# Three edits to the order of work in a two-layer decoder kernel: slot pieces before a routing product, cell transposes one step later, transpose before output in the causal end

## The chip, the cores and the metric

The kernel runs on one core of one Trainium2 chip. The metric is the device time of one execution in microseconds (us), the median of several runs; lower is better. The core has five engines that run side by side and wait for each other through semaphores: PE (TensorE, with its weight loads shown apart as PEld), DVE (VectorE), ACT (ScalarE), POOL (GpSimd) and SP (SyncE, which issues transfers).

## The reference, cut to what matters

Two sequences of 1024 tokens with 256 features (`x`, 16 tiles of 128 tokens) go through two decoder layers. Each of the six blocks adds its result to `x`:

```python
x = x + L0_attn(layernorm(x))            # linear attention and a feed-forward part
x = x + L0_xattn(ctx, layernorm(x))      # queries from x, keys from a context and x itself ("latent")
x = x + L0_ffn(layernorm(x))             # a gated cell scanned over the 2 sequences: "cell"
x = x + L1_attn(layernorm(x))            # causal attention, 16 heads
x = x + L1_xattn(layernorm(x), ctx)      # cross attention, 16 heads
x = x + L1_ffn(layernorm(x))             # 8 experts, top 2 of them per token, at most 64 places per
                                         # group of 256 tokens and expert
```

In the cell, a step is `f*c + i*g` with `f, i = sigmoid(x @ w.T + c @ u.T + b)` and `g = tanh(...)`; its input `x` has to stand feature-major (features on partitions), so the normed rows are transposed first. In the causal block, the attention sums are divided by the sum of the weights and multiplied by `Wout`. In the last block a router (a 256x8 product) gives eight logits per token; softmax, top 2 and a running count per expert then give each token a slot with its experts.

## The kernel before, in words

The stages follow each other in one program: linear attention with its feed-forward part, latent attention, cell, causal attention, cross attention, experts. Wherever it matters here the order of instructions is written out by hand: within `tc.manual_schedule()` each engine takes its instructions in the order in which the Python code issues them (a few short DVE instructions are moved among their neighbours in the build), and generators are stepped against each other so that one stage's side work stands between the steps of another. A wait at the head of an engine's queue holds all that stands behind it on that engine. PSUM tiles come from rings: `k.s()` (two banks each, three of them in the latent, cross and first expert stages, two in the scan), `k.t()` (one bank; three of them in the causal stage); a tile that is taken waits until the tile that had its bank before has been read.

**Cell.norm (L1341 to L1359)** prepares four tiles of 128 tokens for the cell: bn_stats, bn_aggr and a power on POOL (step 1), four `ln_apply` on DVE (L219, step 2), then eight 128x128 transposes on PE (L1355) into one `k.s()` tile and two copies out of it, one on DVE (L1357) and one on ACT (L1358). Each `yield` ends a step. Groups 0 and 1 (the first sequence) run through `Cell.ahead` as the side work of the last unit of latent attention (`Latent.run`, unit 3: `side = following`, one `next(side)` after each of 18 attend steps). An attend step is scores (L1237, with L1226 and L1230 for the context) on PE, an exponential on ACT (L1244), a running sum on DVE (L1249; in the first half of unit 3 always on DVE), and a product (L1164) of an earlier step on PE. Groups 2 and 3 run in `Cell.scan`, one `next(side)` after each of the twelve gates of `Cell.gates` (L1403: four matmuls, then an activation on ACT, L1408; after each three gates DVE combines them, L1414 and L1415). The second sequence's gates (L1439) read groups 2 and 3.

**Causal.finish (L1959 to L2003)** takes each tile t of 128 tokens through three stages: `divide` (four transposes L1968 on PE, reciprocal L1973 and product L1975 on DVE), `turn` (two transposes L1983, copy `yT` L1985 on ACT) and `out` (the product with `wo`, L1991, and the addition to `x` on DVE, L1996). The loop at its end staggers the stages. Each stage is one step of `side` between the attend steps of `Causal.run`; the last four tiles of the second sequence are drained at the end of `Causal.run` with nothing between them. `y` has three buffers, `yT` two.

**CROSS_ORDER (L2071 to L2092)** is a string that names, step by step, the work of the cross attention, with the routing steps of the experts mixed in, and `FIRST_ORDER` (L2477) goes on with the first expert's work. Their names are: `route_<step>_u`, the routing of four tiles, u = 0 to 3: norm, transposes L2600 (`route_turn`), copy `xT` (`route_xT`, L159 on ACT), router product L2608 (`route_prod`), copy of the logits' line (`route_line`), its transposes L2617 (`route_back`), copy into `lg` (`route_copy`, L161 on DVE when the name ends in '); `choose_b`, ten steps that place the tokens of sequence b (L2635 to L2713); `up`, `gelu`, `mul`, a slice of the first expert's hidden layer (L3021 on PE, L3043 on ACT, L3047 on DVE); `scatter_0`, which brings the tokens to their slots. The last two steps of `choose` are 16 short DVE instructions, from `kept` (L2696) to `gate_of` (L2713). The `xT` of routing unit 3 comes from a pool (`moe_route`) that is opened after the pool of the cross attention has been closed and takes its memory, which held the tiles that `choose_0` works on and the `xT` of routing unit 2.

Of the kernel before, what the change touches and what calls it, by code (L numbers as in the profile page):

```python
# [327 lines left out]
class Linear:  # L328
# [79 lines left out]
    def norm(self, g):  # L408
        xh = self.rows4("xh", g)
        for i in range(4):  # L410
            self.k.ln_apply(
                xh[:, i * D : (i + 1) * D], self.group(g)[:, i, :], self.of["mv", g], self.of["r2", g], i
            )
# [286 lines left out]
class Latent:  # L700
# [555 lines left out]
    def finish(self, b):  # L1256

        k, nc, x = self.k, self.k.nc, self.x
        for j in range(2):
            s = k.s()  # L1260
            for i in range(4):
                for c in range(DC):
                    nc.tensor.matmul(
                        s[:, i * D : (i + 1) * D],
                        lhsT=self.oT[(b, j)][:, c, i * P : (i + 1) * P],
                        rhs=self.w["wo"][:, c, :],
                        start=(c == 0),
                        stop=(c == DC - 1),
                    )
            four = x[:, b * TB + 4 * j : b * TB + 4 * j + 4, :]  # L1270
            nc.vector.tensor_tensor(four, four, s.rearrange("p (t d) -> p t d", t=4), ALU.add)
            yield

    def run(self, late, following):
# [43 lines left out]
        drain(side)  # L1318
        finish = self.finish(1)
        next(finish)  # L1320
        self.divide()
        drain(finish)


class Cell:
# [15 lines left out]
    def norm(self, g):  # L1341

        k, nc = self.k, self.k.nc
        rows = lambda i: self.x[:, 4 * g + i, :]
        mv, r = k.ln_stats(rows, 4)
        yield
        xh = self.rows()
        for i in range(4):
            k.ln_apply(xh[:, i, :], rows(i), mv, r, i)
        yield  # L1350
        s = k.s()
        for kc in range(DC):
            for i in range(4):
                at = (kc * 4 + i) * P
                nc.tensor.transpose(s[:, at : at + P], xh[:, i, kc * P : (kc + 1) * P], k.ident)  # L1355
        dst, half = self.xT[g // 2], g % 2 * 512
        nc.vector.tensor_copy(dst[:, 0, half : half + 512], s[:, :512])  # L1357
        nc.scalar.copy(dst[:, 1, half : half + 512], s[:, 512:])  # L1358
        yield  # L1359
# [152 lines left out]
class Causal:  # L1512
# [446 lines left out]
    def finish(self, b, tiles):  # L1959

        k, nc, x = self.k, self.k.nc, self.x
        late = self.late
        ys = {}

        def divide(t):
            s = k.t()
            for grp in range(4):
                nc.tensor.transpose(  # L1968
                    s[:, grp * P : (grp + 1) * P], self.oS[b, t // 4][:, grp, t % 4 * P : (t % 4 + 1) * P], k.ident
                )  # L1970
            s3 = s.rearrange("p (h d) -> p h d", d=32)
            rd = k.small([P, 16], "rd")
            nc.vector.reciprocal(rd, s3[:, :, AUG])  # L1973
            y = ys[t] = late.tile([P, D], F32, tag="y", bufs=3, name="y")
            nc.vector.tensor_tensor(  # L1975
                y.rearrange("p (h d) -> p h d", d=16), s3[:, :, :16], rd.unsqueeze(2).to_broadcast([P, 16, 16]), ALU.mult
            )

        def turn(t):
            y = ys[t]  # L1980
            s = k.t()
            for c in range(DC):
                nc.tensor.transpose(s[:, c * P : (c + 1) * P], y[:, c * P : (c + 1) * P], k.ident)  # L1983
            yT = ys[t] = late.tile([P, D], F32, tag="yT", bufs=2, name="yT")
            nc.scalar.copy(yT, s[:, :D])  # L1985

        def out(t):
            yT = ys.pop(t)
            s = k.t()
            for c in range(DC):  # L1990
                nc.tensor.matmul(  # L1991
                    s[:, :D], lhsT=yT[:, c * P : (c + 1) * P], rhs=self.w["wo"][:, c, :],
                    start=(c == 0), stop=(c == DC - 1),
                )
            one = x[:, b * TB + t, :]
            nc.vector.tensor_tensor(one, one, s[:, :D], ALU.add)  # L1996

        for i in range(len(tiles) + 3):
            for stage, do in ((3, out), (2, turn), (0, divide)):
                if 0 <= i - stage < len(tiles):  # L2000
                    do(tiles[i - stage])
                    yield
# [83 lines left out]
ones_01 sum_3 ones_03 add_2 val_3 inv_3 route_stat_21 route_stat_20 spr_3 os_3 route_mean_2 disp_00  # L2086
route_root_2 yT_3 route_shift_2 route_norm_21' out_3 ones_05 ones_07 route_norm_20' ones_06 ones_04
put_00 disp_01 add_3 route_turn_2 route_stat_31 put_01 route_stat_30 route_xT_2 route_mean_3 up_2
route_root_3 route_prod_2 route_shift_3 route_norm_30' route_norm_31 route_line_2 up_1 route_turn_3
route_back_2 route_copy_2' choose_0 choose_0  # L2090
"""


class Cross:
# [245 lines left out]
    def rows(self, u):  # L2340
        rows = self.tile(u, "mrows", [P, DC, 512], BF16)
        self.k.copy(rows.rearrange("p c n -> p (c n)"), self.of.pop(("m_t", u)))
# [969 lines left out]
```

## Time and profile before

| What | us |
|---|---|
| median of 3 runs | 1535.53 (1532.67 to 1536.07) |
| the profiled execution: its own time | 1539.67 |
| its span in the trace | 1537.70 |
| PE busy in the span | 1498.8 |
| DVE, ACT, POOL busy | 822.1, 502.8, 285.2 |

The profiled execution is one run of its own, 4.1 us above the median of the others; 2.0 us of its time lie outside the span. All durations of the text come from it. A row of the timeline gives start and busy time in us, engine, line, operation, tiles, the number of instructions, and in brackets how long the engine stood idle before the row and what released it. A row of the waits gives the total in us, the number of times and the longest. A row of the windows gives, for a stretch of time, the busy time of PE, PEld, DVE, ACT and POOL, then the clock that PE was granted (1.00 is full speed), the busy share of the DMA engines and GB/s.

### The profile page before, as it was taken

What the parts mean: (1) busy time and instruction counts of PE and PEld (TensorE: products, weight loads), DVE (VectorE), ACT (ScalarE), POOL (GpSimd) and SP (SyncE); (2) the same over time, 40 slices, a digit from 0 to 9 for tenths busy, and PEclk for the clock granted to TensorE, in tenths of its full rate; (3) what the DMA queues carried; (4) which work ended last, traced back from release to release, by engine and by line L of the source; (5) the groups of instructions that cost most, each with busy time, mean ns of one, the idle gap of its engine ahead of it and who ended that gap; (6) DMA issues with size and microseconds to landing.
All of it is one profiled execution on the core that took longest, in us unless ns stands there. A gap on an engine that the chain in (4) does not pass through costs nothing. (4 is left out here: it accounts for less than half of the span.)

```text
span 1537.7 us, 21255 instructions
## 1 busy us (share of the span) xinstructions
PE 1498.8 (97%) x8666; PEld 858.5 (56%) x8672; DVE 822.1 (53%) x1532; ACT 502.8 (33%) x769; POOL 285.2 (19%) x332
## 2 busy tenths in 40 slices
PE   9999999999999999999999999999988999999998
PEld 7765555444343344654444454455677476757786
DVE  6823453656654542587768678367651133343323
ACT  2222411433323332225566645644420111121110
POOL 2002310233212120531511111210033211101110
PEclk9999999999999999999999999999999999999999
DMA  6000000000000000011111111062013275343531
GB/s 260 1 3 1 1 0 0 1 0 1 1 1 0 1 31 1 0 36 56 56 55 56 56 36 60 17 232 63 2 48 129 81 251 193 104 166 122 178 106 56
DMA packets 61378, 94.79 MB, mean 62 GB/s; under 512 B 4616, under 2 KB 52808, under 8 KB 60872
## 3 DMA queue, kind: packets, MB, share of 16 engines
q1 hardware_dynamic: 56216, 80.89, 15.7%
q0 software_dynamic: 3808, 11.05, 2.0%
q8 instruction: 95, 1.56, 0.4%
q10 hardware_dynamic: 1232, 1.07, 0.2%
q14 instruction: 27, 0.22, 0.0%
HBM read 64.13 MB, written 28.87 MB: 60 GB/s over the span
## 5 line engine op out<-in xcount | busy, mean ns | idle before, releaser
L3021 PE MATMUL ps_s<-xe,w 128*128 128x352 f32 (+9 forms) x616 | 171.8, 440 | 0.0
L1951 ACT ACTIVATE pT<-ps_t 128x512 f32<-128x512 f32 x244 | 132.5, 595 | 103.7 <-PE ps_t L1885 103.6
L1768 PE MATMUL ps_s<-kT,qT 32*128 32x512 f32 (+3 forms) x768 | 152.5, 519 | 4.0 <-DVE mneg L1802 2.5
L3047 DVE TENSOR_TENSOR hid<-ga,ps_s 128x512 f32<-128x512 f32 (+3 forms) x99 | 62.0, 628 | 175.8 <-ACT ga L3043 171.5
L1885 PE MATMUL ps_t<-qT,kT 32*128 32x512 f32 (+3 forms) x656 | 150.8, 515 | 0.0
L3060 PE MATMUL ps_o<-wo,hid 128*128 128x256 f32 (+1 forms) x638 | 142.4, 383 | 3.2 <-DVE hid L3047 2.7
L3021 PEld LDWEIGHTS ps_s<-xe,w 128*128 128x128 f32 (+1 forms) x616 | 108.5, 187 | 61.2 <-issue 30.5
L3060 PEld LDWEIGHTS ps_o<-wo,hid 128*128 128x128 f32 (+1 forms) x638 | 121.2, 192 | 22.1 <-DVE hid L3047 3.2
L3043 ACT ACTIVATE ga<-ps_s 128x512 f32<-128x512 f32 (+3 forms) x99 | 54.0, 549 | 207.6 <-PE ps_s L3021 193.6
L1120 DVE TENSOR_REDUCE part<-ps_s 128x2 f32<-128x1024 f32 x64 | 77.3, 1220 | 61.0 <-PE ps_s L1110 60.4
L1244 ACT ACTIVATE pT<-ps_s 128x1024 f32<-128x1024 f32 x64 | 65.5, 1024 | 112.7 <-PE ps_s L1237 112.7
L1802 DVE TENSOR_REDUCE part<-ps_s 128x2 f32<-128x1024 f32 x64 | 77.9, 1221 | 30.0 <-PE ps_t L1885 25.3
L1768 PEld LDWEIGHTS ps_s<-kT,qT 32*128 32x128 f32 x768 | 59.6, 183 | 58.7 <-issue 30.9
L1846 PE MATMUL ps_o<-pT,vr 128*32 128x256 f32 (+1 forms) x1280 | 90.0, 368 | 0.8 <-DVE oS L1861 0.8
L1898 POOL TENSOR_SCALAR_AFFINE_SELECT pT<-pT 128x512 f32<-128x512 f32 (+1 forms) x80 | 44.0, 553 | 231.2 <-ACT pT L1951 211.5
L1802 DVE TENSOR_REDUCE mneg<-ps_s 128x2 f32<-128x768 f32 (+2 forms) x96 | 80.5, 867 | 2.2
L3021 PE MATMUL ps_s<-xin,w 128*128 128x256 f32 (+3 forms) x264 | 78.2, 453 | 3.0 <-DVE hid L3047 3.0
L1249 POOL TENSOR_TENSOR acc<-acc,pT 128x1024 f32<-128x1024 f32 x21 | 49.3, 2349 | 156.9 <-ACT pT L1244 150.7
L1110 PE MATMUL ps_s<-kT,qT 64*128 64x512 f32 x256 | 70.3, 634 | 0.8 <-DVE part L1101 0.8
L1846 PEld LDWEIGHTS ps_o<-pT,vr 128*32 128x32 f32 x1280 | 27.2, 108 | 77.2 <-issue 64.7
L1885 PEld LDWEIGHTS ps_t<-qT,kT 32*128 32x128 f32 x656 | 67.0, 183 | 5.7 <-issue 1.8
L1237 PE MATMUL ps_s<-qT,kT 64*128 64x512 f32 x256 | 68.5, 612 | 1.0 <-DVE part L1120 1.0
(459 smaller groups left out, 2343.2 us busy)
## 6 DMA issues: line engine op xcount, KB each, us to landing
w<-in_w SPq DMA_DIRECT2D x32, 684.0 KB, 8.4
out_rows<-zero SPq DMA_DIRECT2D x7, 2048.0 KB, 7.5
got<-out_rows SPq DMA_DIRECT2D x28, 512.0 KB, 4.8
wo<-in_wo SPq DMA_DIRECT2D x8, 1280.0 KB, 7.0
xi_rows<-xin SPq DMA_DIRECT2D x1, 4112.0 KB
xr<-xi_rows POOLq DMA_DIRECT2D x6, 514.0 KB
w_ffn<-in_w_ffn SPq DMA_DIRECT2D x1, 2304.0 KB
w<-in_w_cell SPq DMA_DIRECT2D x2, 1024.0 KB, 19.1
```

What stands on the lines that cost most here:

```text
L1110: self.k.nc.tensor.matmul(s3[:, hh, :], lhsT=self.q[u][rows, qt * P : (qt + 1) * P], rhs=self.kt[u][rows, half * 512 : (half + 1) * 512], ...
L1120: self.k.nc.vector.tensor_reduce(self.part_of(u)[:, half, qt, :], s3, AX.X, ALU.max, negate=True)
L1237: nc.tensor.matmul(s3[:, hh, :], lhsT=self.ones_h[hr, :] if i else kt[hr, kk * P : (kk + 1) * P], rhs=rows[hr, cols] if i else q[hr, cols] ...
L1244: nc.scalar.activation(pT, s3, AF.Exp)
L1768: self.k.nc.tensor.matmul(s3[:, hh, at : at + n], lhsT=self.q[u][rows, qt * P : (qt + 1) * P], rhs=self.kt[u][rows, half * 512 : half * 51 ...
L1802: nc.vector.tensor_reduce(out, s3[:, :, at : at + n], AX.X, ALU.max, negate=True)
L1846: nc.tensor.matmul(self.o[hh * 32 : hh * 32 + 32, cols], lhsT=self.vr[b][:, kk, 4 * grp + hh, :], rhs=of(hh), start=fresh, stop=last and n ...
L1885: nc.tensor.matmul(out[:, at : at + n], lhsT=kt[rows, kk * P : (kk + 1) * P], rhs=q[rows, j * 512 + q0 : j * 512 + q0 + n], start=True, st ...
L1951: nc.scalar.activation(pT[:, hh, :], heads[hh], AF.Exp)
L3021: self.k.nc.tensor.matmul(cols(s[:m, i * 512 : (i + 1) * 512]), lhsT=wt[:, kc, at : at + m], rhs=cols(self.inputs[e][:, kc, first : 512]), ...
L3047: self.k.nc.vector.tensor_mul(self.hid[:m, hc, first : first + n], self.act.pop(hc)[:m, :n], self.now.pop(hc)[:m, 512 : 512 + n])
L3060: self.k.nc.tensor.matmul(o, lhsT=self.hid[:n, hc, st * P : (st + 1) * P], rhs=self.to[:n, hc, :], start=(hc == 0), stop=(hc == len(HCH) - 1),
```

## The change

Three places of the source change; nothing that is computed does, and the number of instructions on each engine stays the same.

1. `Cell.norm` has one more `yield`, so that the transposes come two steps after the `ln_apply` of their rows instead of one. Where two groups follow each other, all of the second group comes one step later, and its transposes two.
2. The loop at the end of `Causal.finish` takes `turn` before `out`: turn of tile i - 2, out of tile i - 3, divide of tile i.
3. In `CROSS_ORDER` the last two `choose_0` stand before `route_line_2`, ahead of `up_1`, `route_turn_3`, `route_back_2` and `route_copy_2'`, instead of behind them.

```diff
@@ Cell.norm
         for i in range(4):
             k.ln_apply(xh[:, i, :], rows(i), mv, r, i)
         yield
+        yield
         s = k.s()
@@ Causal.finish
         for i in range(len(tiles) + 3):
-            for stage, do in ((3, out), (2, turn), (0, divide)):
+            for stage, do in ((2, turn), (3, out), (0, divide)):
                 if 0 <= i - stage < len(tiles):
                     do(tiles[i - stage])
                     yield
@@ CROSS_ORDER
-route_root_3 route_prod_2 route_shift_3 route_norm_30' route_norm_31 route_line_2 up_1 route_turn_3
-route_back_2 route_copy_2' choose_0 choose_0
+route_root_3 route_prod_2 route_shift_3 route_norm_30' route_norm_31 choose_0 choose_0 route_line_2
+up_1 route_turn_3 route_back_2 route_copy_2'
```

Line numbers of the changed kernel are one higher than those given here from L1351 on.

## The prediction

> **What bounds the kernel now.** I read the page first, then PE's waits, then the timeline around each wait that the change touches. The page says that PE is busy in 97% of the span:
>
> ```profile
> PE 1498.8 (97%) x8666; PEld 858.5 (56%) x8672; DVE 822.1 (53%) x1532; ACT 502.8 (33%) x769; POOL 285.2 (19%) x332
> ...
> PE ps_t L2608 <- ACT xT L159: 4.3, 1, 4.3
> PE ps_s L3021 <- DVE hid L3047: 3.0, 1, 3.0
> PE ps_o L3060 <- DVE hid L3047: 2.7, 1, 2.7
> PE ps_s L1768 <- DVE mneg L1802: 2.5, 6, 0.8
> PE ps_s L1355 <- DVE xh L219: 2.5, 3, 1.3
> ...
> PE ps_t L1991 <- ACT yT L1985: 1.0, 2, 0.5
> ```
>
> The rows below the first are PE's waits in the whole span. So only what PE loses can be won: waits, and matmuls that run slowly because their operands arrive one by one. Three of these rows belong to the three edits: L2608 (router product), L1355 (cell transposes), L1991 (causal output).
>
> **Edit 1, the cell transposes.** Timeline, all in one kernel, the last row for comparison (eight transposes of another stage that wait for nothing between them):
>
> ```profile
> 509.42 1.64 PE L1355 MATMUL ps_s<-ident,xh 128*128 128x128 f32 x8 [0.85 <-DVE xh L219]
> ...
> 519.17 1.65 PE L1355 MATMUL ps_s<-ident,xh 128*128 128x128 f32 x8 [1.26 <-DVE xh L219]
> ...
> 561.74 1.54 PE L1355 MATMUL ps_s<-ident,xh 128*128 128x128 f32 x8
> ...
> 568.79 1.73 PE L1355 MATMUL ps_s<-ident,xh 128*128 128x128 f32 x8 [0.36 <-DVE xh L219]
> ...
> 1108.98 1.04 PE L2600 MATMUL ps_s<-ident,w 128*128 128x128 f32 x8
> ```
>
> Each group waits for the first of four DVE instructions (1.38 us together) and is then paced by the other three: 1.54 to 1.73 us where 1.04 are needed. One step later all four are done. An attend step takes PE 2.29 us (scores at 513.28 and 515.56 in the timeline), a gate 1.72 (four matmuls at 0.43). PE stood ready at 508.57, 517.91, 561.74 and 568.43 (start less wait), and DVE ended its four at 510.24, 520.00, 562.45 and 569.70: late by 1.67 and 2.09 against 2.29, and by 0.71 and 1.27 against 1.72. So all four waits go, the second with only 0.2 us to spare. Gain: 0.85 + 0.60, 1.26 + 0.61, 0.50, 0.36 + 0.69, sum **4.87**. What is late next: the two copies come behind one more running sum (1.22 us) on DVE, and the ACT copy holds the next exponential by some 0.6 us; PE does not need that exponential until a product one step on. A gate's copies stand behind two combining instructions (0.68 + 0.75); group 3 is ready four gates (6.9 us) before L1439 reads it. Bounds: 0 if the later place waits as long for something else, 4.9 at most. I take 4.9, because DVE is late by less than a step in all four rows and its other work keeps its place.
>
> **Edit 3, the slot pieces.** The rows of the L2608 wait, and the same four matmuls one unit earlier at the top:
>
> ```profile
> 1111.83 1.88 PE L2608 MATMUL ps_t<-xT,router 128*8 128x512 f32 x4
> ...
> 1116.44 0.41 PE L2617 MATMUL ps_t<-ident,xT 8*128 8x8 f32 x4
> ...
> 1119.61 0.22 DVE L2713 TENSOR_TENSOR gate_of<-m,m 128x64 f32<-128x64 f32 x1
> 1119.95 1.01 ACT L159 COPY xT<-ps_s 128x1024 f32<-128x1024 f32 x1 [5.57 <-DVE gate_of L2713]
> ...
> 1121.11 3.37 PE L2608 MATMUL ps_t<-xT,router 128*8 128x512 f32 x4 [4.26 <-ACT xT L159]
> ...
> 1124.41 1.59 PEld L3021 LDWEIGHTS ps_s<-xin,w 128*128 128x128 f32 x8 [1.50 <-issue]
> ```
>
> and of the windows
>
> ```profile
> 1122.00:1124.00 2.00, 2.00 (x4) 0.19 (x2) 0.75 (x2) 0.92 (x3) 0.00 (x0) 0.50 0.00 0
> ```
>
> PE is through with `route_back_2` (L2617) at 1116.85 and stands until 1121.11, because ACT's copy takes memory that `choose_0` still reads: `gate_of` is the last of it. The 16 pieces and four `at` instructions among them run from 1116.99 to 1119.83, 2.84 us, and waited only for the `lg` copy ahead of them in DVE's queue. Moved, they begin when DVE has normed unit 3 (two L219, 0.73 us together from 1111.74, done at 1112.47) and end at 1115.3. Then the copy's other wait comes last, the end of L2617 at 1116.85, since `xT` of unit 2 lay in the same memory. With the hand-overs of now (0.12 us to ACT, 0.15 to PE) PE begins L2608 at 1116.85 + 0.12 + 1.01 + 0.15 = 1118.13, 2.98 us earlier, and ends at 1120.01 if the four matmuls take 1.88. Now the next product starts at 1124.41: **4.40** gained, 2.98 of it wait and 1.42 speed. The speed is the clock: the windows row shows 0.50 granted behind this wait. If it falls all the same behind the 1.28 us that remain, the gain is 2.98; that is the lower end where the step works, and 4.4 the upper. I take 4.4, since the waits of 1.26 and 0.85 us above were followed by a clock of 1.00. [...]
>
> What the moved pieces push: on DVE only the `lg` copy (0.19 us, then ready at once at 1116.9); behind it `hid`, which waits for ACT anyway. ACT's table load (1.28) and two gelus follow its copy earlier by 3 us. No transfer is passed: POOL's and SP's queues have the same order in both builds; the scatter's POOL transfers begin earlier with their rows, SP's next weight loads wait for PE (L3021) and move with it.
>
> **Edit 2, transpose before output.** Between attend steps nothing shows: each stage is followed by a whole attend step of PE, and no wait of L1968, L1983 or L1991 stands in the loop; I take 0. In the drain the rows are
>
> ```profile
> 1011.15 1.13 PE L1991 MATMUL ps_t<-w,yT 128*128 128x256 f32 x4 [0.52 <-ACT yT L1985]
> ...
> 1013.02 1.13 PE L1991 MATMUL ps_t<-w,yT 128*128 128x256 f32 x4 [0.52 <-ACT yT L1985]
> ```
>
> where an output directly follows the transpose that feeds it; cross attention's first matmul follows at 1013.99. Behind the third divide (done at 1007.26) PE still has four outputs of 0.97 us from start to start, three turns of 0.22 and one divide of 0.52: 5.06, which would end at 1012.3. In the new order the first turn takes the PSUM bank of the turn before and waits for its ACT copy (1007.36), about 0.2; every other operand is ready a step earlier than needed. End 1012.6, gain **1.4** (0 to 1.7).
>
> **Sum.** 4.9 + 4.4 + 1.4 = 10.7 us. The profiled execution would take 1539.7 - 10.7 = 1529.0 (span 1527.0); the median of the runs, 4.1 below it, **1524.8**, which I predict as 1525. Under 0.2% (3.1 us) a measurement cannot tell from no change.
>
> **Rivals.**
> - *The expert stage gives edits 2 and 3 back.* PE waits there at 1157.07 (2.98) and 1168.95 (2.72, with half clock behind it), because ACT stands 5.34 and 3.14 us for something outside the engines ("remote"). If that event comes at a time of its own, PE reaches the wait earlier and stands longer: only 4.9 remain, 1530.6. Against it: POOL's and SP's transfers hang on DVE and PE and move along. The same rows can fall better: without these two waits and the half clock some 5 us more would go, 1520.
> - *The cell gain is not there*: the transposes wait in the new place too, for a DVE that is behind with its sums (1.22 us in every step of that half, plus statistics of 1.93 us, 1.40 + 0.36 + 0.17). 5.8 remain, 1529.7. Against it: DVE is busy 20.84 of the 40 us from 500.
> - *The clock falls behind the shorter wait too*: 1.4 less, 1526.2.
> - *Little is left*: both of the first two at once, under 3 us, 1533.
> - *Slower*: in the loop of causal attention a stage takes the bank that the stage before it leaves. Now divide waits for the addition L1996 (turn does so before), and turn for the division's product (output before). If DVE, which has a 1.23 us reduction in front of it in nearly every step, answers later than the next step begins, each of 12 tiles costs one such reduction, 14.8 us: 1539.3 against 1535.5. It decides from 0.9 us per tile. Against it: PE's waits show no such row in the loop now, although the banks are handed on at the same distance of one step.
>
> **How the numbers follow.** Forecast 0.69 (its own range 1522 to 1528: 1 us on each edit and 2 of scatter of the median of three). Expert stage takes it back 0.10, falls better 0.05; no cell gain 0.05; clock 0.04; little left 0.04; slower 0.03. Faster by over 0.2%: 0.69 + 0.10 + 0.05 + 0.05 + 0.04 = 0.93; same 0.04; slower 0.03. The range for 8 in 10 reaches from the better to the worse expert stage, 1520 to 1531.
>
> **What would show it.** Edit 1: four groups of L1356 at about 1.04 us without a wait. Edit 3: the copy of `xT` released by PE L2618, L2609 at 1.88 us after a wait near 1.3, clock 1.00. Edit 2: no wait of L1992 for `yT`, cross attention's first matmul 1.4 us sooner after the last `oS` copy. It is wrong if PE's busy time and waits fall by 10 us up to 1125 but the end moves less (the expert stage), or if new waits stand at L1969, L1984 or L1992 between the attend steps.

## The result, and the profile after

The changed kernel takes 1522.13 us (median of 4 runs, 1521.57 to 1524.38) against 1535.40 of the kernel before beside it (4 runs): ratio 0.9923, 95% interval 0.991 to 0.9935, or 11.8 us (10.0 to 13.8). The medians lie 13.3 us apart. Predicted were 1525.0 us and 10.7 us. The profiled execution after took 1524.38 us, its span 1522.3 against 1537.7: 15.4 us. Where the span fell by more than the runs is the question that the prediction left to its rivals, and the experiments answer it.

In all rows after, lines from L1351 on are one higher than before. The page's first part, then PE's waits in the span (engine, tile, line, released by: total, times, longest):

```profile
PE 1495.5 (98%) x8672; PEld 860.4 (57%) x8672; DVE 821.8 (54%) x1532; ACT 503.0 (33%) x769; POOL 284.8 (19%) x332
```

```profile
PE ps_s L1769 <- DVE mneg L1803: 2.5, 6, 0.8
...
PE ps_t L2609 <- ACT xT L159: 1.2, 1, 1.2
...
PE ps_o L3061 <- DVE hid L3048: 0.9, 1, 0.9
```

The rows of the cell transposes (2.5) and of the causal output (1.0) are gone, the wait for `xT` is 1.2 and not 4.3, and the only new row is one of 0.5 us at L3022 ("issue": nothing that the profile shows held it), which the second profile of this kernel below does not have. The first gated product no longer waits for `hid` (3.0 before), and the first product with `wo` waits 0.9 and not 2.7; no edit was priced for that.

The four groups of cell transposes, in the timeline after:

```profile
511.23 1.09 PE L1356 MATMUL ps_s<-ident,xh 128*128 128x128 f32 x8
...
521.38 1.21 PE L1356 MATMUL ps_s<-ident,xh 128*128 128x128 f32 x8
...
560.66 1.04 PE L1356 MATMUL ps_s<-ident,xh 128*128 128x128 f32 x8
...
568.40 1.04 PE L1356 MATMUL ps_s<-ident,xh 128*128 128x128 f32 x8
```

None waits. Three need the 1.04 to 1.09 us of transposes whose operands are all there; the second group, for which the prediction had 0.2 us to spare, is 0.17 us over 1.04.

The wait for the last `xT`:

```profile
1109.83 0.22 DVE L2714 TENSOR_TENSOR gate_of<-m,m 128x64 f32<-128x64 f32 x1
...
1111.25 0.41 PE L2618 MATMUL ps_t<-ident,xT 8*128 8x8 f32 x4
...
1111.74 1.01 ACT L159 COPY xT<-ps_s 128x1024 f32<-128x1024 f32 x1 [2.55 <-PE ps_t L2618]
...
1112.89 1.88 PE L2609 MATMUL ps_t<-xT,router 128*8 128x512 f32 x4 [1.24 <-ACT xT L159]
...
1114.70 1.99 PE L3022 MATMUL ps_s<-xin,w 128*128 128x256 f32 x8
```

`gate_of`, the last slot piece, now ends 1.2 us ahead of L2618. The copy is released by the end of L2618, which reads the older `xT` in the same memory; the four products behind it take 1.88 and not 3.37 us.

The end of the causal drain, two rows of before and then the rows after:

```profile
1006.46 0.44 PE L1983 MATMUL ps_t<-ident,y 128*128 128x128 f32 x2 [0.37 <-DVE y L1975]
...
1013.99 1.00 PE L2184 MATMUL ps_s<-w 96*128 96x64 f32 x8
```

```profile
1001.46 0.44 PE L1984 MATMUL ps_t<-ident,y 128*128 128x128 f32 x2 [0.38 <-DVE y L1976]
...
1005.41 1.89 PE L1992 MATMUL ps_t<-w,yT 128*128 128x256 f32 x8
1007.14 1.00 PE L2185 MATMUL ps_s<-w 96*128 96x64 f32 x8
```

The last two outputs run as one row of eight products, without the two waits of 0.52 us. From the L1984 that waits for `y` to cross attention's first matmul it is 5.68 us; before it was 7.53.

**Where PE is ahead.** I follow PE's starts through both traces and take off that the execution after began its latent stage 0.44 us late (the product L1164 at 480.99 against 480.55). PE leads by 3.23 us at L1263 (553.46 before, 550.67 after), by 4.97 when the scan is over, 5.44 in the drain (1006.46 and 1001.46) and 7.29 at cross attention's first matmul. Then it loses 1.64 us to a stretch at half clock, and by the last router product it gains 4.51: 12.58 us from the start of L2608 of unit 2 to the product after that of unit 3 before (1111.83 to 1124.41), 8.07 after (1106.63 to 1114.70). Edit 1 has given 4.97 us, edit 2 2.3 and edit 3 4.5, together 11.8. The other 5.9 us of the lead over the span arise behind 1125, in the expert stage. Whether each of the three gains belongs to its edit is what the experiments test.

### The profile page after: what moved, and what is told of

Read it like the earlier page. It is cut to its first block, busy times and chain, and to the rows that moved or that the text cites. A ratio compares the mean times of both kernels' runs of the same rounds, so it can differ in the third digit from the quotient of the medians.

```text
span 1522.3 us, 21261 instructions
## 1 busy us (share of the span) xinstructions
PE 1495.5 (98%) x8672; PEld 860.4 (57%) x8672; DVE 821.8 (54%) x1532; ACT 503.0 (33%) x769; POOL 284.8 (19%) x332
## 3 DMA queue, kind: packets, MB, share of 16 engines
q10 hardware_dynamic: 1232, 1.07, 0.2%
## 5 line engine op out<-in xcount | busy, mean ns | idle before, releaser
L3022 PE MATMUL ps_s<-xe,w 128*128 128x352 f32 (+9 forms) x616 | 172.3, 441 | 0.5 <-issue 0.5
L3022 PEld LDWEIGHTS ps_s<-xe,w 128*128 128x128 f32 (+1 forms) x616 | 108.6, 188 | 62.1 <-issue 31.9
L3022 PE MATMUL ps_s<-xin,w 128*128 128x256 f32 (+3 forms) x264 | 77.8, 452 | 0.0
```

The costliest lines, as they stand in the source:

```text
L3022: self.k.nc.tensor.matmul(cols(s[:m, i * 512 : (i + 1) * 512]), lhsT=wt[:, kc, at : at + m], rhs=cols(self.inputs[e][:, kc, first : 512]), ...
```

## The experiments

Theory: the three edits add, each by the PE time that it frees. Main rival: the expert stage decides, so that a part of the gain hangs on when PE comes to it. In the accounts below a profile's start is taken off as above, and 1.6 us for every stretch at half clock. Each kernel is compared with runs of the kernel before that were made beside it on the same chip.

### One edit at a time

Cell transposes alone:

```diff
@@ Cell.norm
         yield
+        yield
```

> Only the cell transposes one step later; the causal end and the slot pieces as before. Theory (the three edits add, each by the wait it takes away): the four groups of transposes run in about 1.04 us without a wait, PE is 3.2 us ahead when the causal half begins and 5.0 us ahead (4.95) at its end, and keeps that to the end: 1530.5 against 1535.4. The wait of 4.26 us for the slot pieces and the outputs waiting for yT in the causal end stand as before. Rival (the expert stage decides): the lead meets an event of its own time in the expert stage, and the end moves by under 2 or by over 7 us.

Measured: 1528.71 us against 1534.54, ratio 0.996 (0.9944 to 0.9975). PE leads by 3.23 us at L1263 and by 4.97 at cross attention's first matmul; the waits of 4.26 us for `xT` and 0.52 (twice) for `yT` stand as before. The 4.97 us are edit 1's, and nothing gives them back; the ratio's interval, 3.8 to 8.6 us, holds them, with the median on its better side.

Output order alone:

```diff
@@ Causal.finish
-            for stage, do in ((3, out), (2, turn), (0, divide)):
+            for stage, do in ((2, turn), (3, out), (0, divide)):
```

> Only the order of turn and output in the causal end (drain and loop); the rest as before. Theory: the drain is 1.9 us shorter, as the trace after shows, and the loop 0.45 us: 1533.0 against 1535.4 if both belong to this edit; 1533.5 if the 0.45 us is something else. Rival of the prediction (banks handed on in the loop): waits of turn or divide between the attend steps, up to 14.8 us, 1550; the trace after speaks against it. Second rival: the 1.9 us came from reaching the causal end earlier, then nothing changes here.

Measured: 1532.15, ratio 0.998 (0.9968 to 0.9992). PE leads by 2.27 us at cross attention's first matmul. No wait of turn, output or divide stands between the attend steps, so the slower rival has no row to rest on; and the second one, by which nothing would change here, falls with the 2.27 us.

Slot pieces alone:

```diff
@@ CROSS_ORDER
-route_root_3 route_prod_2 route_shift_3 route_norm_30' route_norm_31 route_line_2 up_1 route_turn_3
-route_back_2 route_copy_2' choose_0 choose_0
+route_root_3 route_prod_2 route_shift_3 route_norm_30' route_norm_31 choose_0 choose_0 route_line_2
+up_1 route_turn_3 route_back_2 route_copy_2'
```

> Only choose_0 choose_0 ahead of route_line_2; the rest as before. Theory: PE's wait for xT falls from 4.26 to about 1.25 us and the matmuls behind it run at full clock, 1.88 us: 4.5 us, 1530.9 against 1535.4. Rival (the 2 to 3 us that the whole change won in the expert stage belong to this edit, since the pieces start its transfers earlier): 1528 to 1529, with no wait of the first gated product for hid. Rival (the stands of ScalarE there are chance of an execution): 1531, and the waits for hid appear in some profiles and not in others.

Measured: 1529.87, ratio 0.9966 (0.9951 to 0.9982). The wait is 1.24 us and the products take 1.88; from L2608 of unit 2 (1114.78) to the product after unit 3 (1122.85) it is 8.07 us as in the whole change, 4.51 less than before. The three medians add up to 5.8 + 2.4 + 4.7 = 12.9 us. The first product does not wait for `hid` here, but it does not in the two kernels above either, which leave edit 3 out: those waits do not belong to this edit.

### What holds the copy: memory or data

None of the three edits, only another place for the last `xT`:

```diff
@@ Cross.__init__
+        self.qk = wt[:, : 4 * D].rearrange("p (c n) -> p c n", c=DC)
@@ Cross.run
-        moe.route = route[-1]
+        moe.route, moe.xT3 = route[-1], self.qk
@@ Experts.scores
-        pool, bufs = (pool, 2) if u < 2 * B - 1 else (self.fp, 1)
-        xT = pool.tile([P, DC, 512], F32, tag="xT", bufs=bufs, name="xT")
+        xT = pool.tile([P, DC, 512], F32, tag="xT", bufs=2, name="xT") if u < 2 * B - 1 else self.xT3
```

> Order as before, none of the three edits; the last routing unit's xT lies in memory that the query and key weights of cross attention left, no longer in the memory that the slot pieces read. It tells whether the memory or the order of the data made the copy wait. Theory (memory): the copy starts behind the transposes L2600 alone, PE waits about 0.9 us and not 4.26, and the matmuls run at full clock: 4.8 us, 1530.7, no less than the moved pieces give, although the pieces still stand behind. Rival (ScalarE or VectorE come to it late whatever the memory): the wait stays near 4.3 us, 1535.4.

Measured: 1531.58, ratio 0.9973 (0.996 to 0.9987). Its timeline (`xT` is called `w` here; the transposes L2600 stand at L2601, the other lines as before):

```profile
1116.13 1.01 ACT L159 COPY w<-ps_s 128x1024 f32<-128x1024 f32 x1 [2.17 <-PE ps_s L2601]
...
1117.19 1.88 PE L2608 MATMUL ps_t<-w,router 128*8 128x512 f32 x4 [0.76 <-ACT w L159]
...
1119.20 0.23 DVE L2713 TENSOR_TENSOR gate_of<-m,m 128x64 f32<-128x64 f32 x1
1119.52 1.28 ACT L3043 ACT_TABLE_LOAD   x1 [2.38 <-DVE gate_of L2713]
...
1121.97 0.41 PE L2617 MATMUL ps_t<-ident,w 8*128 8x8 f32 x4 [0.97 <-ACT w L159]
```

The copy starts 3.3 us ahead of the end of `gate_of`, released by the transposes alone: the memory was what held it, not the data. From L2608 (1111.41) to the next product (1119.01) it is 7.60 us, 4.98 less than before. But ACT's next work still stands until `gate_of` is done (third and fourth row), and the copy of the logits comes behind it: a new wait of 0.97 us that the expectation had not seen. What stays is 4.0 us in the profile. The expectation, 4.8 us and no less than the moved pieces give, was missed; the median has 3.0 us against their 4.7.

The same edit on the changed kernel, that is the diff of the change and the one above together:

> The whole change, and besides the last routing unit's xT in the memory of cross attention's query and key weights. Theory: PE's wait for xT falls from 1.24 to 0.76 us as in the kernel with its own memory alone, 0.5 us better than the change, 1521.7; the wait of 0.97 us that stood there before the next L2617 does not come back, since ScalarE no longer stands until the slot pieces are done. Rival (it comes back, since ScalarE takes the gelu first): 1522.7 or more, no better than the change.

Measured: 1520.85 against 1534.22, ratio 0.9921 (0.9905 to 0.9936). The wait for `xT` is 0.76 us, L2618 of unit 3 does not wait, and the stretch of 8.07 us is 7.60: 0.47 us better in the profile. The medians are too coarse for half a microsecond: in its own comparisons the changed kernel itself stands at 0.9923 and 0.9912.

### Each part of edits 1 and 2

Groups 0 and 1 alone, then groups 2 and 3 alone:

```diff
@@ Cell.norm
         yield
+        if g < 2:
+            yield
```

```diff
@@ Cell.norm
         yield
+        if g >= 2:
+            yield
```

> Only the cell transposes of groups 0 and 1 one step later (those beside the latent attention); groups 2 and 3, the causal end and the slot pieces as before. Theory: 3.2 us by the two waits (0.85, 1.26) and their stretched groups, and besides, in the executions in which the clock fell to half for 3.41 us behind the 1.26 us wait (it did so in two of the five profiles that have this wait), another 1.6 us: 1531.3 by the waits alone, about 1530.5 in the median. Rival (nothing but the waits counts): 1531.3, with the granted clock spread over the executions as before the change.

> Only the cell transposes of groups 2 and 3 one step later (those beside the causal scan); the rest as before, so the waits of 0.85 and 1.26 us stand. Theory: 1.74 us by the waits, 1532.8 against 1534.5, and no change of the clock; with the kernel that moves groups 0 and 1 it adds up to what moving all four gave (5.8). Rival (the scan hides it): 1534.5.

Measured: 1530.22, ratio 0.9978 (0.9965 to 0.9991), and 1532.65, ratio 0.9987 (0.9979 to 0.9996), both against 1534.22. In the profiles PE leads by 3.24 and by 1.76 us, the terms of the theory. Of the half clock behind the 1.26 us wait, the expectation counted one profile too many; it was two of four at that time, and it is two of seven now:

```profile
520.00:524.00 4.00, 4.00 (x15) 1.58 (x15) 1.66 (x2) 0.92 (x2) 0.00 (x0) 0.57 0.00 0
```

This is the windows row of the kernel with the output order alone, granted clock 0.57 behind that wait. That the median of the first kernel wins by it is not shown: its runs had clocks from 0.993 to 0.999, those of the kernel before 0.992 to 0.999.

The drain's order alone:

```diff
-    def finish(self, b, tiles):
+    def finish(self, b, tiles, end=False):
...
-            for stage, do in ((3, out), (2, turn), (0, divide)):
+            for stage, do in ((2, turn), (3, out), (0, divide)) if end else ((3, out), (2, turn), (0, divide)):
...
-        drain(self.finish(1, range(TB // 2, TB)))
+        drain(self.finish(1, range(TB // 2, TB), True))
```

> Only the last causal drain has turn ahead of output; the loop keeps the old order, and the rest is as before. Theory: the drain wins 1.9 us as with the full edit, and the 0.4 us that the full edit won besides lie in the loop, so the lead over before is 1.9 us at cross attention's first matmul, 1532.6 against 1534.5. Rival (the 0.4 us come from elsewhere): 2.3 us here too.

Measured: 1531.81, ratio 0.9984 (0.9972 to 0.9995). PE leads by 1.86 us at cross attention's first matmul, against 2.27 with the full edit. So 0.4 us lie in the loop: in the full edit they appear between 891 and 936 us, where neither kernel has a row of waits. PE's starts show where. In the kernel before, behind the turn at 886.26:

```profile
885.89 1.08 ACT L1951 ACTIVATE pT<-ps_t 128x512 f32<-128x512 f32 x2 [2.01 <-PE ps_t L1885]
...
886.64 1.08 PE L1885 MATMUL ps_t<-qT,kT 32*128 32x512 f32 x2
```

The score products L1885 take their tiles from the same ring `k.t()` as the stages, so that a stage which takes one of its three banks leaves them one that is still in use. The second one of this row starts 0.39 us behind the first, at 887.03, when ACT's exponential has read the bank that it takes (886.98); where none is late, such a row is 0.70 us long. No wait is listed, since the first product still runs. From the first scores behind a stage (L1768) to the product L1846 it takes 1.07 us where none is late. Behind a turn it takes 1.44 us in the mean of eight, in both profiles of before and with the drain's order alone. With the full edit it is 1.34 in seven turns and 1.07 in the eighth, while it grows from 1.14 to 1.23 behind the six divides. Over the 22 stages of this stretch that is 26.92 us before, 26.93 with the drain's order alone and 26.47 with the full edit: the 0.4 us. Why the new order shortens these holds was not tested apart.

### Is the rest of the gain in the expert stage the kernel's

The two kernels of the comparison once more, with no edit:

> The kernel before, unchanged, for a second profile. Theory (the three stands of ScalarE, 11.3 us together, and PE's two waits for hid, 2.98 and 2.72 us, are chance of one execution): this profile has the wait of L3021 gone and that of L3060 near 0.9 us, and a span near 1533, 4 to 5 us under the first profile, with the wait of 4.26 us and the half clock behind it as they were. Rival (they belong to the kernel before): they stand again at the same place, and the span is near 1537.

> The kernel after, unchanged, for a second profile and a tighter median. Theory (the half clock at 1086 without any wait is chance): 1522.3 us; the profile shows the same waits as the first, the half clock at another place or not at all, and a span of 1520.6 if there is none. Rival (it belongs to the small matmuls there): the half clock stands at the same place.

Measured: the kernel before 1535.25 us (ratio to its own other runs 0.9991, 0.9979 to 1.0003), the kernel after 1523.36, ratio 0.9912 (0.9894 to 0.993). In the first profile of before ACT stood idle three times, 11.3 us in all, and the trace names no engine that released it ("remote"):

```profile
1153.44 0.38 ACT L3043 ACTIVATE ga<-ps_s 128x256 f32<-128x256 f32 x1 [2.85 <-remote]
1159.16 0.94 ACT L3043 ACTIVATE ga<-ps_s 128x256 f32<-128x256 f32 x3 [5.34 <-remote]
...
1170.78 0.38 ACT L3043 ACTIVATE ga<-ps_s 88x256 f32<-88x256 f32 x1 [3.14 <-remote]
```

In the second one it stands nowhere in this way; its gelus follow each other every 1.72 us:

```profile
1170.56 0.38 ACT L3043 ACTIVATE ga<-ps_s 128x256 f32<-128x256 f32 x1 [1.34 <-PE ps_s L3021]
1172.28 0.38 ACT L3043 ACTIVATE ga<-ps_s 88x256 f32<-88x256 f32 x1 [1.34 <-PE ps_s L3021]
```

The wait of L3021 is gone, that of L3060 is 0.9, as expected of the theory. Followed like the other kernels, this profile gains 6.9 us on the first profile of the same kernel between 1145 and 1180 us, and so does the first profile of the kernel after (the half clock behind the 2.7 us wait is counted in). The span, 1537.6, is not the 1533 that I expected, for another reason: this execution spent 20.5 us ahead of its end at half clock, the first profile 6.8. The second profile of after has no half clock except at its very end, and a span of 1519.0. So the waits for `hid` are not the kernel before's; its first profile paid them, and the profile after did not.

### The last of the wait

The transposes of the last unit ahead of a product, first on the changed kernel, then with `xT` in its own memory too:

```diff
@@ CROSS_ORDER
-up_1 route_turn_3 route_back_2 route_copy_2'
+route_turn_3 up_1 route_back_2 route_copy_2'
```

> The whole change, and besides the last unit's transposes (route_turn_3) ahead of the product up_1, so that 1.83 us of products stand between them and route_back_2; xT stays in the memory that route_back_2 reads. Theory (memory: the copy waits for the end of L2618, not for the transposes): the wait of 1.24 us stands as it was, 1522.5. Rival (the copy follows the transposes): the copy runs beside the products and the wait goes, 1521.2.

> The same order (route_turn_3 ahead of up_1) on the kernel with the whole change and xT in memory of its own. Theory: now nothing but the transposes holds the copy (1.01 us and two hand-overs of 0.1 to 0.15), it is done beside the products (1.83 and 0.41 us), and PE does not wait for xT of the last unit at all: 0.76 us better than with its own memory alone, 1520.1 to 1520.5. Rival (turned earlier, the transposes wait for the normed rows): a new wait at L2601.

Measured: 1528.32 and 1528.34 against 1540.21, ratios 0.9921 (0.9908 to 0.9935) and 0.9916 (0.9901 to 0.9931). The first one's timeline:

```profile
1112.94 1.01 ACT L159 COPY xT<-ps_s 128x1024 f32<-128x1024 f32 x1 [2.51 <-PE ps_t L2618]
1114.10 1.88 PE L2609 MATMUL ps_t<-xT,router 128*8 128x512 f32 x4 [1.24 <-ACT xT L159]
```

and the second one's:

```profile
1112.70 1.01 ACT L159 COPY w<-ps_s 128x1024 f32<-128x1024 f32 x1 [0.39 <-PE ps_s L2602]
...
1114.32 0.41 PE L2618 MATMUL ps_t<-ident,xT 8*128 8x8 f32 x4
1114.66 1.88 PE L2609 MATMUL ps_t<-w,router 128*8 128x512 f32 x4
```

With the old memory the earlier transposes win nothing; the copy still starts behind L2618. With its own memory it runs beside the product, PE goes from L2618 to L2609 without a gap, and the stretch from L2609 of unit 2 to the product after unit 3 is 6.72 us, where the first one has 8.02. Again the medians do not show it. Both absolute times miss the expectation by 6 to 8 us, and that bears on the question of the expert stage: on this chip the kernel before took 1538.08 us at least (1532.45 to 1532.85 on the three other chips of the experiments), and in both profiles ACT stands again, twice, as in the first profile of before (the first one's rows):

```profile
1150.48 0.94 ACT L3044 ACTIVATE ga<-ps_s 128x256 f32<-128x256 f32 x3 [5.29 <-remote]
...
1162.10 0.38 ACT L3044 ACTIVATE ga<-ps_s 88x256 f32<-88x256 f32 x1 [3.12 <-remote]
```

PE's waits for `hid` are 2.9 and 2.7 us here, in kernels that have all three edits. So these idle times of ACT seem to go with the chip, as far as ten profiles without them on three chips and two with them on this one can show. They do not go with the change: the second profile of before lacks them, these two kernels with all three edits have them, and the ratios on this chip are those of the others. My theory of a chance of one execution is not borne out, and its rival falls. The chip of the first profile of before is not on record, no kernel before was profiled on this chip, and what ACT waits for is not in the traces.

## Why the prediction was right

**Edit 1** was priced at 4.87 us and gave 4.97: 3.23 in the latent stage (priced 3.32) and 1.74 in the scan (1.55). The step "DVE is late by less than a step in all four rows" held, and so did the tightest row of it.

**Edit 3** was priced at 4.40 and gave 4.51. Wait 1.24 us (predicted 1.28), released by L2618, 1.88 us at clock 1.00: each link of the chain as worked out. The rival that the clock falls behind the shorter wait did not come: no profile has half clock behind the waits of 1.24 us (four profiles) or 0.76 (two).

**Edit 2** was mis-sized, in the drain and in the loop. The drain was priced at 1.4 us and gave 1.85. The failed term is its end, "at 1012.3" and with the bank 1012.6. In the trace after, the same work takes 5.68 us from the waiting L1984; set at 1006.46 it ends at 1012.14. The wait for the bank came as the text had it: the turn behind the third divide is released by ACT's copy at 1002.37, some 0.2 us late; the sum had added 0.3. What was too dear is the work behind it, 4.73 us and not 5.06, because the four outputs took 3.57 us from start to start (0.87, 0.97 and 1.73 for the last two together) and not 4 x 0.97.

The loop was priced at 0, on the ground that no wait of L1968, L1983 or L1991 stands there, and gave 0.4. That step failed: the banks of the stages hold the score products up, 0.37 us behind a turn, without a row of waits.

**The sum** by the traces is 11.8 us against 10.7, of which edit 2 has 0.9; the ratio of the runs gives the same 11.8. The other 1.5 us between the medians are within its interval. The step that mattered most was to take the gain off the profiled execution and to carry its 4.1 us over the median along unchanged: the 5.9 us by which the two spans differ in the expert stage are no part of the change. The prediction had no second profile to tell this from, and gave "falls better" 0.05; that it left them out came true, but it had not been shown.

**The rivals.** The expert stage neither gave back nor fell better by the change; what looked in the profile after like the rival "falls better" came in the second profile of the kernel before too. The slower one, banks in the loop, has no row of waits in any of the kernels with the new order; what there is of it, 0.09 us more behind a divide, is less than what the turns win. Its time was a slip: 12 reductions on 1524.8 give 1539.6, not 1539.3.

## What to carry to other kernels

A wait can be held by memory that a tile inherited: ask whether the waiting instruction reads what its releaser wrote, and if not, either end the old readers earlier or give the tile another place; giving it another place frees only what stood for that memory, and ACT's next instruction may still stand (2.38 us in the kernel with `xT` in its own memory). Price a re-ordering by what PE gets back, wait and stretched matmuls together, row by row; and look at the starts of a stage's instructions before it is priced at nothing, since a hold shorter than the work in flight has no row of waits (0.37 us behind a turn here). Before the rest of a difference between two profiles is put down to a change, take both profiles again: half-clock stretches (6.8 and 20.5 us ahead of the end in the two profiles of before) and ACT's idle times without a releaser at its gelus (11.3 us and none) differed between the profiles here by more than most of these edits bring.

## What the runs showed of the hardware

- In the traces every stretch at half clock ahead of the end is 3.41 us long or a multiple (6.83, 10.24), and one of 3.41 cost PE 1.64 us in the profile after.
- In these runs the length of a wait alone did not tell whether the clock fell: a stretch at half clock followed the 4.26 us wait in all seven profiles that have it, but also the 2.7 us wait in all three that have it, and the 1.26 us wait in two of seven. None followed the wait of 2.9 to 3.0 us in the same three.
- It came in three of the fourteen profiles without any wait, each time at the end of the same ten pairs of small matmuls (outputs of 128x32, 0.39 us a pair), PE being busy throughout. In the profile after it falls at 1086.28, 0.4 us behind the last pair; in its second profile not at all. The same place three times speaks for a part of these matmuls in it, but no run takes them away, and what decides is open:

```profile
1086.00:1088.00 2.00, 2.00 (x13) 0.45 (x13) 1.86 (x13) 0.00 (x0) 0.00 (x0) 0.57 0.00 0
```

- Three profiles, of the kernels with the turn ahead (both) and of the second one of before, have 10.24 us at half clock in cross attention (from 1027 to 1037 us on). They begin just behind two waits of 0.7 and 0.6 us, which the other profiles have too, and PE is busy in them. What brings it is open. The second profile of before also has one stretch near its start, at 12.55 us, in a wait of 1.41 us.
